# Close's products one chunk later, a third buffer for split's scaled copies, and a norm chain over three chunks

## The chip, the cores and the metric

The kernel runs on one core of one Trainium2 chip. The core has TensorE (PE, matmuls; its weight loads are listed as PEld), VectorE (DVE), ScalarE (ACT), GpSimd (POOL) and SyncE (SP), which here only issues DMAs. Each takes its own instructions in order, and they meet through semaphores. The metric is the device time of one execution in microseconds, as the median of several runs.

## The reference

Four images of 96 channels by 128 x 128 pixels, all in float32, pass through two layers, each added to its input after a group norm (`_gn`). The first is a state-space block: a projection and depthwise convolution to 192 channels, four scans over the pixels (`y0` to `y3`), their sum, a layer norm over the 192 channels at each pixel, and a projection back:

```python
ym = (y0 + y1 + y2 + y3).reshape(B, D_INNER, H, W)
yn = jnp.moveaxis(ym, 1, -1)
yn = (yn - mu) * jax.lax.rsqrt(var + 1e-05) * ln_w + ln_b
yn = jnp.moveaxis(yn, -1, 1)
return jnp.einsum('bdhw,cd->bchw', yn, out_w) + out_b[None, :, None, None]
...
x = x + _L0_conv_ref(_gn(x), ...)
```

The second layer splits its input by sign, makes convolution weights of the two halves ("attention"), and joins the results:

```python
xr, x1, x2 = _relu_split_norm(x, sc1, sc2, res_coef, nc1, nc2)
y1 = NORM_SCALE * _layer_norm(_attn_conv(x1, x2, aw1, aw2, aw3))
y2 = NORM_SCALE * _layer_norm(_conv2d(x2, w_conv2, K // 2)) * x1
y = jnp.concatenate([y1, y2], axis=1)
return xr + _conv2d(y, w_full, 0) + b_full[None, :, None, None]
```

## The kernel before

The program is one unrolled stream, written as Python generators that emit instructions and yield a cost in units. `co_run(left, right, pace)` takes a step of `left` and then as many steps of `right` as make up its cost times `pace`; this sets the order in which two tasks are emitted. In the first part, up to the end of the scan, `in_order` fixes on each engine the order of emission. After that the compiler's planner places instructions by its own estimate of times, with the order of emission as priority, so neighbours on one engine can change places. A tile in a pool with `bufs` buffers shares them with its successors; the writer of a new tile waits until all users of the tile that had the buffer are done (a WAR wait).

The stages are: projections and scan of all images; norm, count and split of image 0 beside the end of the scan; its maps by direct convolution (L2138), with image 1's norm beside it; then for each image the attention (`left`: products L1507 and L1522, evacuated by ACT as `odd` and `ends` at L1578 and by DVE at L1592 to L1600), beside a chain of light work (`right`): the norm of the next image, its count, and then its split in turn with the close of the image before. At the start of images 2 and 3 what is left of the light chain is emitted alone (`drain(light)`). Image 3 has a last stage of its own.

- **Norm** (`ssm_output`, L937). It walks over NS = 16 chunks of SN = 1024 pixels in six sections a round. `load_y` brings y, 96 partitions x 2 halves of the channels x 1024, from DRAM, into 3 buffers. `squares` (ACT, L956) and `sums` (PE, L966) make the sums over channels of y and of its squares; `rows` copies them out (ACT, L975) and turns them into `mq`, 8 partitions x 128, by two DMAs. `inverse` (DVE, L982 to L984), `roots` (ACT, L988) and `back` (DVE, L994 or L999; a store to `rd` on POOL's queue, L1001; a load of the input `xr` on SP's, L1003) give the inverse root, and `spread_out` (POOL's queue, L1009) loads it on all partitions as `r`. `projected` (PE, L1015) multiplies y by the output weights, a half of 512 pixels at a time, `scaled` (DVE, L1028, L1030) multiplies by r, `added` (POOL, L1036, L1038) adds xr, `counted` (DVE, L1042) takes statistics, and L1091 stores the chunk. Round c serves chunk c as `new`, c − 1 as `mid` and c − 2 as `old`. A round's six yields come to 8.2 units, and all of it to 149.6. For images 1 to 3 (`turned`) the sum lies in r's buffer, for image 0 in xr's. mq, xr and r have two buffers each.
- **Split** (`split_pieces`, L1219) makes two halves of the input for 32 pieces of four rows, and from each half six planes (`planes_of`, L1407): ACT makes two scaled copies, `x4` (L1430, three buffers) and `x2` (L1431, two buffers), and POOL forms the differences (L1439 to L1444, L1425).
- **Close** (`attn_output`, L2266) walks over NCH = 32 chunks of 512 pixels in three sections. `loads` brings `o`, `c2` and `xx` of the next chunk by three DMAs on SP's queue; ACT makes `x1` and `e` from xx (L2308), DVE finishes x1 (L2312), c2 (L2313) and e (L2316, L2317), PE adds two products into one PSUM bank (L2319 of o, L2320 of c2), DVE adds e (`added`, L2298 or L2300), and SP stores it (L2301). c2, xx, x1, e and o have two buffers each. `added` comes in the next chunk, ahead of its x1.

Norm's sums and projections, split's halves and close's products share two PSUM banks in `psr`.

Of the kernel before, what the change touches and what calls it, by code (L numbers as in the profile page):

```python
# [9 lines left out]
F32 = mybir.dt.float32  # L10
BF16 = mybir.dt.bfloat16
AF = mybir.ActivationFunctionType
# [5 lines left out]
C = 96  # L18
H = W = 128
L = H * W  # L20
CH = 512
NCH = L // CH
# [29 lines left out]
SN = 1024  # L52
# [17 lines left out]
def kernel(  # L70
# [211 lines left out]
    def part(ps, *shape):  # L282
        n = 1
        for d in shape[1:]:
            n *= d
        t = bank(ps)[: shape[0], :n]
        return t if len(shape) == 2 else t.rearrange("p (a b) -> p a b", b=shape[2])
# [649 lines left out]
    def ssm_output(b, yms, xnew, stats, ps, side, turned):  # L937
# [5 lines left out]
        with tc.tile_pool(name="c2", bufs=2, side=side) as p2:  # L943
            xb = x[b].rearrange("c h w -> c (h w)")
            ym = yms.rearrange("(j p) l -> p j l", j=2)
            rd = dram.tile([L], F32, name="rd")
            ys, sums_of, near, made = {}, {}, {}, {}

            def load_y(c):
                if c < NS:  # L950
                    ys[c] = p2.tile([C, 2, SN], F32, name="y", bufs=3)
                    nc.sync.dma_start(ys[c], ym[:, :, bass.ts(c, SN)])

            def squares(c, j):
                sq = p2.tile([C, SN], F32, name="sq")
# [55 lines left out]

            def projected(c, h):
                po = part(ps, C, CH)
                for j in range(2):
                    nc.tensor.matmul(  # L1015
                        po,
                        lhsT=outws[:, j],
                        rhs=ys[c][:, j, bass.ts(h, CH)],
                        start=(j == 0),
                        stop=(j == 1),  # L1020
                    )
                return po
# [18 lines left out]
                t = near[c][turned]  # L1041
                nc.vector.bn_stats(stats[:, 2 * c + h], t[:, bass.ts(h, CH)])  # L1042

            for c in range(3):
                load_y(c)
            yield 2.0
            for c in range(NS + 2):
                new, old = c < NS, c - 2 if c >= 2 else None
                mid = c - 1 if 1 <= c <= NS else None
                if old is not None:  # L1050
                    po = projected(old, 0)
                if mid is not None:
                    inverse(mid)
                if new:
                    squares(c, 0)
                yield 1.2
                if mid is not None:
                    roots(mid)
                if old is not None:
                    scaled(old, 0, po)  # L1060
                    po = projected(old, 1)
                    ys.pop(old)
                if new:
                    squares(c, 1)
                yield 1.4
                if mid is not None:
                    back(mid)
                if old is not None:
                    added(old, 0)
                    scaled(old, 1, po)  # L1070
                if new:
                    sums(c, 0)
                yield 1.4
                if new:
                    sums(c, 1)
                if old is not None:
                    added(old, 1)
                    counted(old, 0)
                    load_y(c + 1)
                yield 1.4  # L1080
                if new:
                    rows(c)
                if mid is not None:
                    xr = near[mid][0]
                    nc.scalar.activation(xr, xr, AF.Identity, bias=outbs)
                    spread_out(mid)
                if old is not None:
                    counted(old, 1)
                yield 1.4
                if old is not None:  # L1090
                    nc.sync.dma_start(xnew[:, bass.ts(old, SN)], near.pop(old)[turned])  # L1091
                yield 1.4

    def split_count(xnew, stats, keep, cnt, ps, side):
# [124 lines left out]
    def split_pieces(pools, xnew, x1d, x2d, keep, cnt, ps, side, planes, done):  # L1219
# [20 lines left out]
        def stored(i, m, h):  # L1240
            if planes:
                def then(pl):
                    store_planes(nc.sync, m, i * rows, rows, pl)
                    done[m is x2d] = (i + 1) * rows

                return planes_of(later, p2, h, rows, then, rows, bufs=(3, 2, 3), wait=1)
            at = (i * rows + 1) * PW
            return lambda: nc.scalar.dma_start(m[:, at : at + rows * PW], h)

# [1016 lines left out]
    def attn_output(pools, img, ps, side, share):  # L2266

        ob = out[img.b].rearrange("c h w -> c (h w)")  # L2270
        p1 = pools.enter_context(tc.tile_pool(name="f1", bufs=1, side=side))
        p3 = pools.enter_context(tc.tile_pool(name="f3", bufs=2, side=side))
        with_one = [p1.tile([128, CH], F32, name=f"o{k}")[0 : C + 1] for k in range(2)]
        for o in with_one:
            nc.gpsimd.memset(o[C : C + 1], 1.0)
        cost = 2.6 / 3 * share

        def loads(t):
            if t == NCH:
                return None  # L2280
            o = with_one[t % 2]
            got = [o]
            nc.sync.dma_start(o[0:C], img.od[:, bass.ts(t, CH)])
            for name, src in (("c2", img.c2d), ("xx", img.xnew)):
                y = p3.tile([C, CH], F32, name=name)
                nc.sync.dma_start(y, src[:, bass.ts(t, CH)])
                got.append(y)
            return got

        ahead = loads(0)  # L2290
        w1 = own_weights(img, ps, p1)
        s2, w2 = c2_weights(img, ps, p1)
        thr, scale, shift, up, low = (img.keep[n] for n in ("thr", "scale", "shift", "up", "low"))
        stt = nc.vector.scalar_tensor_tensor

        def added(t, pf, x1, e):
            if img.mapped:
                nc.vector.tensor_add(x1, pf, e)  # L2298
            else:
                nc.vector.tensor_add(plain(x1), pixels(pf), pixels(e))  # L2300
            nc.sync.dma_start(ob[:, bass.ts(t, CH)], x1)  # L2301

        summed = None
        for t in range(NCH):
            o, c2, xx = ahead
            x1, e = (p3.tile([C, CH], F32, name=n) for n in ("x1", "e"))
            for y, m, s in ((x1, scale[:, 0:1], shift[:, 0:1]), (e, up[:, 0:1], up[:, 1:2])):
                nc.scalar.activation(y, xx, AF.Identity, scale=m, bias=s)  # L2308
            yield cost
            if summed:  # L2310
                added(*summed)
            stt(x1, xx, thr, x1, ALU.is_gt, ALU.mult)  # L2312
            stt(c2, c2, s2[0:C, 0:1], x1, ALU.subtract, ALU.mult)  # L2313
            ahead = loads(t + 1)
            yield cost
            stt(e, xx, thr, e, ALU.is_gt, ALU.mult)  # L2316
            stt(e, xx, low[:, 0:1], e, ALU.mult, ALU.add)  # L2317
            pf = part(ps, C, CH)
            nc.tensor.matmul(pf, lhsT=w1, rhs=o, start=True, stop=False)  # L2319
            nc.tensor.matmul(pf, lhsT=w2, rhs=c2, start=False, stop=True)  # L2320
            summed = t, pf, x1, e
            yield cost
        added(*summed)

    class LastOutput:

# [363 lines left out]
```

## Time and profile before

| | us |
|---|---|
| median of 3 runs | 6667.03 |
| lowest and highest run | 6646.25, 6669.15 |
| profiled execution, its own time | 6658.24 |
| its span, first to last instruction | 6656.4 |

| stage (by its instructions in the trace) | window, us |
|---|---|
| norm of image 0, beside the scan | 2095 to 2360 |
| norm and count of image 1, beside the direct maps | 3215 to 3540 |
| norm of image 2, beside the attention of image 1 | 3950 to 4250 |
| split of image 2 with close of image 0 | 4311 to 4880 |
| norm of image 3, beside the attention of image 2 | 4880 to 5180 |
| split of image 3 with close of image 1 | 5260 to 5710 |
| close of image 2, beside the attention of image 3 | 5710 to 6130 |

The mean granted clock of PE is 0.879 of full speed over the span. The DMA engines moved 1198.45 MB, at a mean of 180 GB/s. A line of waits names the engine and the line that waited, what released it, the total, the number of times and the longest. In a line of a group the part after the first bar is its busy time and its mean in ns, and that after the second the idle time of the engine just ahead of it, with what ended it.

### The profile page before, as it was taken

The page shows a single profiled execution, that of the slowest core. Times are in us where ns is not written, and L with a number is a line of the kernel's source. Part 1 is how long each engine was busy: PE and PEld are TensorE (multiplying, and loading weights), DVE is VectorE, ACT ScalarE, POOL GpSimd, SP SyncE. Part 2 cuts the span into 40 slices and gives each one's busy share as a digit, 9 for nine tenths or more (in the row PEclk, how much of TensorE's full clock was granted, in tenths as well). Part 3 has the DMA queues.
Part 4 walks back from the last instruction along what each step waited for, and adds up shares of the span by engine and source line. Part 5 has one row for each costly group of instructions (what it writes and reads, how often), then busy time and mean ns, then how long its engine had stood idle before and what let it go on. Part 6 is the DMA issues. An engine that isn't in the chain of part 4 may idle for free. (4 is left out here: it accounts for less than half of the span.)

```text
span 6656.4 us, 78702 instructions
## 1 busy us (share of the span) xinstructions
PE 5402.4 (81%) x23264; PEld 2361.0 (35%) x23264; DVE 4808.8 (72%) x7229; ACT 3931.9 (59%) x5141; POOL 3963.2 (60%) x4145
## 2 busy tenths in 40 slices
PE   6889978978887727999984778877869777888888
PEld 2333323322222103444332243444324444344553
DVE  3247878988998778889557555676755777788867
ACT  1257768777876676677324664655645655644542
POOL 2236758978787548889325684388454577533420
PEclk9999989988997758999987889887979888998989
DMA  7766777865766766765765757545756554755657
GB/s 164 176 157 176 208 212 195 226 181 170 225 186 171 213 183 207 212 187 179 202 181 156 202 152 189 156 130 161 212 158 164 154 144 133 228 152 157 182 148 213
DMA packets 972215, 1198.45 MB, mean 180 GB/s; under 512 B 221518, under 2 KB 801686, under 8 KB 959308
## 3 DMA queue, kind: packets, MB, share of 16 engines
q1 hardware_dynamic: 948172, 1138.48, 61.7%
q0 software_dynamic: 16208, 38.42, 2.1%
q10 hardware_dynamic: 7408, 16.53, 0.8%
q8 instruction: 187, 3.06, 0.2%
q14 instruction: 240, 1.97, 0.1%
HBM read 777.62 MB, written 345.58 MB: 169 GB/s over the span
## 5 line engine op out<-in xcount | busy, mean ns | idle before, releaser
L635 PE MATMUL bank<-y,wp 128*128 128x512 f32 (+3 forms) x3584 | 1312.3, 622 | 80.7 <-DMA y<-y 33.3
L868 POOL TENSOR_TENSOR y<-y,dl 128x1024 f32<-128x1024 f32 x384 | 1064.5, 2772 | 263.6 <-DVE dl L860 238.1
L835 POOL TENSOR_TENSOR dl<-dl,u 128x1024 f32<-128x1024 f32 x384 | 1015.1, 2643 | 246.6 <-ACT dA L811 123.0
L856 DVE TENSOR_TENSOR_SCAN dA<-dA,pBC 128x512 f32<-128x512 f32 x768 | 981.5, 1278 | 30.7
L1507 PE MATMUL two<-ya,wd 128*64 128x192 f32 (+3 forms) x2376 | 609.8, 434 | 170.1 <-ACT odd L1578 83.9
L749 PE MATMUL pBC<-xr,wbc 60*128 60x512 bf16 (+1 forms) x1536 | 461.6, 403 | 322.8 <-DVE dA L856 248.1
L635 PEld LDWEIGHTS bank<-y,wp 128*128 128x128 f32 (+3 forms) x3584 | 457.5, 168 | 747.2 <-issue 651.4
L2138 PE MATMUL bank<-y,wn 128*128 128x384 f32 (+5 forms) x2408 | 675.3, 505 | 57.9 <-DMA y<-x1d 28.5
L860 DVE TENSOR_TENSOR dl<-dA,pBC 128x512 f32<-128x512 f32 x768 | 528.1, 688 | 252.6 <-PE pBC L749 180.0
L1941 ACT COPY yb<-ya 64x768 f32<-64x768 f32 (+1 forms) x660 | 537.1, 814 | 200.7 <-PE two L1507 143.7
L678 ACT ACTIVATE dl<-pd,dtb 128x512 f32<-128x512 f32 x768 | 485.5, 684 | 191.4 <-PE pd L749 173.8
L1507 PE MATMUL two<-yb,wd 128*64 128x192 f32 (+3 forms) x2376 | 582.2, 416 | 0.2 <-ACT yb L1941 0.2
L839 DVE TENSOR_TENSOR pBC<-dl,pBC 128x512 f32<-128x512 f32 x768 | 527.6, 687 | 8.8 <-POOL dl L835 7.7
L1425 POOL TENSOR_TENSOR pl<-x 96x128 f32<-96x128 f32 (+1 forms) x1032 | 496.7, 494 | 0.0
L2138 PEld LDWEIGHTS bank<-y,wn 128*128 128x128 f32 (+3 forms) x2408 | 310.2, 168 | 352.4 <-issue 177.3
L811 ACT ACTIVATE dA<-dl,negA 128x1024 f32<-128x1024 f32 x384 | 420.3, 1141 | 2.3
L1507 PEld LDWEIGHTS two<-ya,wd 128*64 128x64 f32 (+1 forms) x2376 | 275.3, 175 | 405.8 <-issue 113.9
L2011 POOL COPY own<-ring 32x512 f32<-32x512 f32 (+1 forms) x198 | 221.3, 1152 | 287.4 <-DVE ring L1600 253.0
L749 PEld LDWEIGHTS <-wbc 60*128 60x128 bf16 (+1 forms) x1536 | 104.1, 96 | 763.0 <-issue 750.0
L678 ACT ACT_TABLE_LOAD x248 | 318.2, 1283 | 93.9 <-PE pd L749 81.9
L1507 PEld LDWEIGHTS two<-yb,wd 128*64 128x64 f32 (+1 forms) x2376 | 304.7, 175 | 157.7 <-issue 49.8
L1507 PE MATMUL two<-ya,wa 128*96 128x384 f32 (+1 forms) x528 | 235.2, 530 | 111.0 <-DMA ya<-vp 57.5
(324 smaller groups left out, 10067.8 us busy)
## 6 DMA issues: line engine op xcount, KB each, us to landing
u<-zb SPq DMA_DIRECT2D x192, 1024.0 KB
yms<-y SPq DMA_DIRECT2D x96, 512.0 KB
y<-yms SPq DMA_DIRECT2D x64, 768.0 KB
ya<-vp SPq DMA_DIRECT2D x120, 336.0 KB
y<-y SPq DMA_DIRECT2D x128, 258.2 KB
zb<-z SPq DMA_DIRECT2D x64, 512.0 KB
xn<-xnew SPq DMA_DIRECT2D x80, 384.0 KB
ya<-x1p SPq DMA_DIRECT2D x90, 336.0 KB
```

The costliest lines, as they stand in the source:

```text
L635: nc.tensor.matmul(blocks(pz[p:e]), lhsT=ws[k][:, d, c : c + e - p], rhs=window(ys[k], at, d, n), start=(i == 0), stop=(i == len(terms) - 1),)
L678: nc.scalar.activation(dst, src, AF.Softplus, bias=bias)
L749: nc.tensor.matmul(p, lhsT=w[rows], rhs=xr[rows, at : at + CH], start=True, stop=True)
L835: nc.gpsimd.tensor_mul(t, t, u_view(n))
L839: nc.vector.tensor_mul(p, live[n]["dl"][:, bass.ts(half, CH)], p)
L856: nc.vector.tensor_tensor_scan(h, h, p, init, ALU.mult, ALU.add)
L860: nc.vector.tensor_mul(live[n]["dl"][:, sl], live[n]["dA"][:, sl], live[n]["C", half])
L868: nc.gpsimd.tensor_add(v, v, t.rearrange("p (a b) -> p a b", b=W))
L1425: op(to[i], x, y)
L1507: nc.tensor.matmul(of(to[p:e], r), lhsT=w[:, i, c : c + e - p], rhs=tiles(t[k][PAIR[i]][:, SLOT[i]], o, r), start=(k == 0), stop=False,)
L1941: nc.scalar.copy(yb[k][64 * h - 64 : 64 * h, :, :n], ya[k][0:64, :, h * TN : h * TN + n])
L2138: nc.tensor.matmul(pc[p:e, :n].rearrange("p (h w) -> p h w", w=W), lhsT=w[:, c : c + e - p], rhs=v[:, :, 0:W], start=(i == 0), stop=(i == ...
```

## The change

In the norm, y has two buffers for the squares and the sums, loaded a whole round ahead. A second read, `load_half`, brings y again in halves of 512 pixels (`yh`, two buffers of half the size) for `projected`. A round now serves four chunks: `new` c, `mid` c − 1, `far` c − 2 and `old` c − 3. `inverse`, `roots`, `back` and `spread_out` stand in other sections, `rows` and the first `counted` in the last; the second `counted` comes in the next round. A round costs 7.8 units, there is one more, and the whole is 153.3. In the split, x2 has three buffers. In the close the two products of a chunk come at the start of the next one, `added` behind that chunk's c2, and `loads` a section later.

```diff
@@ ssm_output
-            ys, sums_of, near, made = {}, {}, {}, {}
+            ys, again, sums_of, near, made = {}, {}, {}, {}, {}
             def load_y(c):
                 if c < NS:
-                    ys[c] = p2.tile([C, 2, SN], F32, name="y", bufs=3)
+                    ys[c] = p2.tile([C, 2, SN], F32, name="y")
                     nc.sync.dma_start(ys[c], ym[:, :, bass.ts(c, SN)])
+            def load_half(i):
+                if i < NCH:
+                    again[i] = p2.tile([C, 2, CH], F32, name="yh")
+                    nc.sync.dma_start(again[i], ym[:, :, bass.ts(i, CH)])
...
             def projected(c, h):
                 po = part(ps, C, CH)
+                y = again.pop(2 * c + h)
...
-                        rhs=ys[c][:, j, bass.ts(h, CH)],
+                        rhs=y[:, j],
...
-            for c in range(3):
+            for c in range(2):
                 load_y(c)
-            yield 2.0
-            for c in range(NS + 2):
-                new, old = c < NS, c - 2 if c >= 2 else None
+                load_half(c)
+            yield 4.0
+            late = []
+            for c in range(NS + 4):
+                new = c < NS
                 mid = c - 1 if 1 <= c <= NS else None
+                far = c - 2 if 2 <= c <= NS + 1 else None
+                old = c - 3 if 3 <= c <= NS + 2 else None
+                if c > NS + 2:
+                    yield 1.1
+                    late.pop()()
+                    return
+                if far is not None:
+                    back(far)
                 if old is not None:
                     po = projected(old, 0)
-                if mid is not None:
-                    inverse(mid)
                 if new:
+                    if c:
+                        load_y(c + 1)
                     squares(c, 0)
-                yield 1.2
-                if mid is not None:
-                    roots(mid)
+                yield 1.1
                 if old is not None:
                     scaled(old, 0, po)
                     po = projected(old, 1)
-                    ys.pop(old)
+                if late:
+                    late.pop()()
                 if new:
                     squares(c, 1)
-                yield 1.4
+                yield 1.3
                 if mid is not None:
-                    back(mid)
+                    inverse(mid)
+                if far is not None:
+                    spread_out(far)
                 if old is not None:
                     added(old, 0)
                     scaled(old, 1, po)
...
                     sums(c, 1)
                 if old is not None:
                     added(old, 1)
-                    counted(old, 0)
-                    load_y(c + 1)
-                yield 1.4
+                    load_half(2 * old + 2)
+                yield 1.3
+                if mid is not None:
+                    roots(mid)
+                if far is not None:
+                    xr = near[far][0]
+                    nc.scalar.activation(xr, xr, AF.Identity, bias=outbs)
+                if old is not None:
+                    load_half(2 * old + 3)
+                yield 1.3
                 if new:
                     rows(c)
-                if mid is not None:
-                    xr = near[mid][0]
-                    nc.scalar.activation(xr, xr, AF.Identity, bias=outbs)
-                    spread_out(mid)
                 if old is not None:
-                    counted(old, 1)
-                yield 1.4
-                if old is not None:
-                    nc.sync.dma_start(xnew[:, bass.ts(old, SN)], near.pop(old)[turned])
+                    counted(old, 0)
+                    nc.sync.dma_start(xnew[:, bass.ts(old, SN)], near[old][turned])
+                    late.append(lambda old=old: (counted(old, 1), near.pop(old)))
                 yield 1.4
@@ split_pieces
-                return planes_of(later, p2, h, rows, then, rows, bufs=(3, 2, 3), wait=1)
+                return planes_of(later, p2, h, rows, then, rows, bufs=(3, 3, 3), wait=1)
@@ attn_output
-        def added(t, pf, x1, e):
+        def multiplied(o, c2):
+            pf = part(ps, C, CH)
+            nc.tensor.matmul(pf, lhsT=w1, rhs=o, start=True, stop=False)
+            nc.tensor.matmul(pf, lhsT=w2, rhs=c2, start=False, stop=True)
+            return pf
+        def added(pf, t, x1, e):
...
-        summed = None
+        behind = None
         for t in range(NCH):
             o, c2, xx = ahead
...
+            if behind:
+                pf = multiplied(*behind[0])
             yield cost
-            if summed:
-                added(*summed)
             stt(x1, xx, thr, x1, ALU.is_gt, ALU.mult)
             stt(c2, c2, s2[0:C, 0:1], x1, ALU.subtract, ALU.mult)
+            if behind:
+                added(pf, *behind[1])
+            yield cost
             ahead = loads(t + 1)
-            yield cost
             stt(e, xx, thr, e, ALU.is_gt, ALU.mult)
             stt(e, xx, low[:, 0:1], e, ALU.mult, ALU.add)
-            pf = part(ps, C, CH)
-            nc.tensor.matmul(pf, lhsT=w1, rhs=o, start=True, stop=False)
-            nc.tensor.matmul(pf, lhsT=w2, rhs=c2, start=False, stop=True)
-            summed = t, pf, x1, e
+            behind = (o, c2), (t, x1, e)
             yield cost
-        added(*summed)
+        pf = multiplied(*behind[0])
+        yield cost
+        added(pf, *behind[1])
```

## The prediction

> **What bounds the kernel now.** I read the shares first, then windows cut at the stages, then the waits of TensorE (PE) in those windows, last the groups of single lines.
>
> ```profile
> PE 5402.4 (81%) x23264; PEld 2361.0 (35%) x23264; DVE 4808.8 (72%) x7229; ACT 3931.9 (59%) x5141; POOL 3963.2 (60%) x4145
> ...
> 2095.00:2360.00 265.00, 191.25 (x498) 46.53 (x497) 186.23 (x250) 172.14 (x188) 146.09 (x103) 0.67 0.74 210
> 3215.00:3540.00 325.00, 274.64 (x1027) 113.48 (x1024) 160.20 (x417) 114.06 (x176) 76.47 (x130) 0.89 0.68 182
> 3950.00:4250.00 300.00, 259.87 (x1442) 124.47 (x1444) 167.22 (x308) 142.26 (x186) 139.78 (x183) 0.91 0.64 171
> 4311.00:4880.00 569.00, 443.40 (x2050) 230.23 (x2048) 408.31 (x667) 328.21 (x502) 399.55 (x773) 0.81 0.58 164
> 4880.00:5180.00 300.00, 244.18 (x1316) 113.05 (x1316) 163.88 (x303) 138.28 (x180) 140.84 (x171) 0.89 0.62 166
> 5260.00:5710.00 450.00, 343.45 (x1860) 198.07 (x1861) 335.98 (x504) 248.39 (x383) 350.54 (x659) 0.82 0.51 147
> 5710.00:6130.00 420.00, 374.15 (x1751) 186.67 (x1749) 338.80 (x548) 226.19 (x315) 159.35 (x261) 0.93 0.61 176
> ```
>
> Columns of a window: length, busy time of PE, PE's weight loads, DVE, ACT and POOL, granted clock, DMA share, GB/s. Windows 1, 2, 3 and 5 hold the norm of images 0 to 3, windows 4 and 6 split beside close (images 2 and 0, then 3 and 1), window 7 mostly the close of image 2. PE leads, but is idle 74, 50, 40, 126, 56, 107 and 46 us there: 499 us, all that the change can win. Between 2440 and 3215 us and in the attention alone nothing is touched.
>
> ```profile
> PE bank L2320 <- DVE c L2313: 54.5, 17, 15.5
> ...
> PE bank L2320 <- DVE c L2313: 33.0, 11, 8.5
> PE two L1507 <- ACT odd L1578: 28.4, 7, 9.8
> ...
> PE bank L2320 <- DVE c L2313: 22.2, 16, 4.6
> ...
> PE bank L966 <- ACT sq L956: 23.5, 9, 4.5
> ...
> PE bank L966 <- DMA y<-yms: 18.6, 2, 14.8
> ```
>
> These are PE's waits (total us, times, longest) in windows 4, 6, 7, 1 and 5. Close's second product waits for c2: 54.5 + 33.0 + 22.2 = 109.7 us, 44 times. PE works in order, so the attention's products stand behind it.
>
> ```profile
> L2312 DVE SCALAR_TENSOR_TENSOR x<-xx,kept,x 96x512 f32<-96x512 f32 x96 | 150.5, 1567 | 69.4 <-ACT x L2308 63.4 <-DMA out<-x 5.4
> L1431 ACT ACTIVATE x<-half 96x264 f32<-96x264 f32 x192 | 81.6, 425 | 198.5 <-POOL pl L1444 198.2
> L982 DVE TENSOR_TENSOR mq<-mq 8x128 f32<-8x128 f32 x64 | 42.0, 656 | 160.0 <-DMA mq<-st 136.4 <-DMA yc<-x1p 23.5
> ```
>
> Each ends in the idle time ahead of it: c2's own operand is slow (L2312 has a mean of 1567 ns, a median of 748, a maximum of 11016), split's second scaled copy stalls ACT for 198 us, norm's first step on mq stalls DVE for 160 us.
>
> [...] one shape (L1015) takes 590 to 1170 ns, and the clock is lowest (0.81, 0.82) where PE waits most. [...] from the end of xx's issue to its first reader there are never under 2.8 us.
>
> **Close.** Nothing is added; the two products move from the third section of a chunk to the first of the next, the add behind x1's and c2's two DVE operations (1.5 us at 748 ns), and the three loads one section later. A section lasts 5.8, 6.3 and 2.9 us in the three closes (96 starts of L2308). c2 is then made two sections ahead of its product, 5.8 to 12.6 us, more than all but one of the 44 waits: I take 109.7 us off PE's list. What is late next:
> - DVE still loses the time in L2312. PE runs ahead only until the attention wants its next PSUM pair, freed by the same ACT and DVE queues. Give back 40%: +44 (between 0 and 110).
> - xx has a section less. I paired the 96 xx issues with their L2308 in time: the lead has a median of 12.6, 12.2 and 6.7 us. Taking a section off each lead, and letting ACT wait where less than 3.1 us is left, gives +87 us of ACT idle. ACT is 54 to 58% busy, so I pass 30% on: +26 (0 to 87).
> - [...] I take −10 (−20 to 0).
>
> Net −110 + 44 + 26 − 10 = −50, between −130 and +87. On SP the out store (L2301) is now behind a later add, and the loads behind that store; PE's WAR release of o and c2 keeps its two sections.
>
> **Third buffer.** One more x2 lets ACT write a copy three halves behind POOL's reading instead of two. x4 has three already, so the next limit is L1430, one instruction earlier. ACT's wait was 68.1 + 69.2 + 14.1 us in windows 4, 6, 7; half should go. What reaches PE is `odd` coming late, 7.9 + 6.7 and 28.4 + 5.8 us in windows 4 and 6, with other causes too; a quarter: −12 (−49 to +5[...]).
>
> **Norm.** PE's waits that belong to it, windows 1, 2, 3, 5: for sq 23.5 + 1.3 + 7.9 = 32.7, for y 3.2 + 7.8 + 2.1 + 18.6 = 31.7, for r (L1028, L1030) 18.2; 82.6 together. Distances between a step and its user, in the yields' units (one is 1.8 us: L956 advances 14.8 us a chunk of 8.2 units in window 3):
> - mq's DMA to its first DVE step 2.8 to 3.8; that step to the root 1.2 to 2.7; sums to rows 1.4 to 2.6; xr's load to its bias 2.8 to 5.1; r's load to scaled 4.0 to 6.5. ACT's waits ahead of L988 (139.6 us), L975 (115.2) and L1085 (59.3), and DVE's 144.6 for mq and 62.4 for r, should fall by well over half. The root no longer stands ahead of the second square: sq −22, r −10.
> - y to squares 4.2 to 7.8: −32. But projected now reads yh, loaded 4.0 and 3.8 units ahead, where y had 4.2 and was late 17 times on ACT and 7 on PE: give back half, +16. The WAR releases are early: yh's by a product two sections before.
> - The slot of r: from the store that frees it to spread_out 6.8 to 3.8 units, about 7 us. POOL waited 21.2 us for this store before; three times that stalls POOL, not PE, but attention's L2011 stands behind: +5. For image 0 the slot of xr frees only when counted has run, one section after its load is issued, so SP stands there 2.5 us a chunk, ahead of the scan's prefetches, which are several steps early: +3.
> - DVE comes earlier to the scan's and attention's steps: window 1 has 30.4 us of PE waiting for dA (L856); −5.
> - y is read twice: 12.6 MB more an image, 128 issues instead of none, some 0.4 us each on SP. At 171 to 210 GB/s the DMA share of these windows goes from 0.62–0.74 to about 0.8–0.92; +5 for later landings (0 to 40).
> - A 19th round: 153.3 units for 149.6, 3.7 × 1.8 = 7 us an image of one stream, shown only where that stream is emptied alone (4805 to 4880): +5.
>
> Net −22 − 10 − 32 + 16 + 5 + 3 − 5 + 5 + 5 = −35, between −88 and +60.
>
> **Sum.** −50 − 12 − 35 = −97. From this I take 10 off for the planner: after image 0's part instructions are placed by its own estimate (in the timeline at 4061 us L966's products of y precede L1015's, those of sq follow), so a section isn't a fixed place. −87 on 6658.24 (span 6656.4 and 1.8 around it) is 6571. The median shown, 6667.03, is 8.8 higher, and its runs spread over 22.9; I forecast 6575.
>
> **Rivals.**
> - *Waits change their name, no change.* PE stops waiting for c2 and waits for `odd` and the PSUM pairs instead. For: window 4 has DVE and POOL at 72 and 70%, and DVE waits 47.6 us for `odd` there. Against: window 7, with POOL at 38%, shows c2 waits too. Close gives 10 and norm 10: about 6645. Chance 0.22. That placement undoes the delay (a product put back beside its operand) ends here too.
> - *Everything is won.* 110 + 20 from close, 60 from norm, 20 from split: about 6475. Chance 0.08.
> - *Slower: close's loads become the loop.* xx's landing (3.1), L2308 (0.8), x1 (0.75), c2 (0.74), the add (1.05), the store's issue (0.4), three issues (1.4) now follow one another, as the loads stand on SP behind the store of an add that stands behind this chunk's c2: 8.2 us a chunk with no queue ahead. Window 7's chunk lasts 8.8 us, so 0.6 us of queueing decides. If a load loses two sections, the same pairing gives 293 us of ACT idle instead of 87; 75% of it on PE against the 110 won is +110, less 20 from the rest: about 6760. For: SP's stores already hang behind DVE (89.8 us at L2301 in window 7). Against: the planner may issue the loads ahead of the store, since o and c2 are free by then. Chance 0.25.
>
> **Numbers.** The forecast has 0.45 (own range 6530 to 6620). About 0.5% (33 us) is what a measurement of this kernel tells from no change. Faster: 0.45, 0.08 and a little of the first rival, 0.55; same 0.18; slower 0.27. The range, 6465 to 6750, leaves out the worse half of the slower case and a little at the lower end.
>
> **What would show it.** L2320's wait for c2 under 15 us; L2308's wait for xx 12.1 before, under 100; L1431's for POOL under 110; L982's for mq under 70; L966's for y near nothing and L1015 with a new wait for yh of 10 to 25; windows 4 and 6 shorter by 20 us each, clock above 0.84. Wrong: L1507's waits for `odd` up by more than 60 us, L2308's above 200, or the closes' chunk above 8.8 us in the last.

## The result, and the profile after

The changed kernel takes 6745.56 us (median of 4 runs, 6743.37 to 6765.72) against 6666.57 us for the kernel before: ratio 1.0132, interval [1.0104, 1.016]. The change is slower by about 1.3%; the forecast was 1.4% faster. A second measurement beside its parts gave 1.0133. The profiled execution has a span of 6742.2 us and a granted clock of 0.874, before 6656.4 us and 0.879. The engines' busy times in it:

```profile
PE 5408.8 (80%) x23264; PEld 2368.4 (35%) x23264; DVE 4727.9 (70%) x7229; ACT 3933.0 (58%) x5140; POOL 3985.0 (59%) x4145
```

PE is busy as long as before (5402.4 us), so what was lost is idle time of PE.

The stage windows of after, in the order of the seven shown for the kernel before (length, busy time of PE, weight loads, DVE, ACT and POOL, clock, DMA share, GB/s):

```profile
2095.00:2400.00 305.00, 186.67 (x506) 48.25 (x506) 180.06 (x264) 175.90 (x195) 148.89 (x104) 0.63 0.81 224
3240.00:3600.00 360.00, 283.94 (x1078) 122.07 (x1078) 165.53 (x393) 99.71 (x152) 91.42 (x126) 0.87 0.76 201
4060.00:4380.00 320.00, 270.50 (x1514) 136.74 (x1512) 167.34 (x329) 145.87 (x192) 138.68 (x170) 0.90 0.72 189
4440.00:4985.00 545.00, 428.92 (x1935) 216.30 (x1931) 373.83 (x646) 316.99 (x483) 404.40 (x763) 0.83 0.62 172
4990.00:5300.00 310.00, 272.94 (x1515) 136.95 (x1507) 165.22 (x327) 145.26 (x191) 144.62 (x179) 0.90 0.76 199
5365.00:5800.00 435.00, 344.11 (x1789) 189.39 (x1789) 300.07 (x494) 247.06 (x380) 352.59 (x647) 0.82 0.56 153
5800.00:6220.00 420.00, 368.41 (x1751) 184.46 (x1752) 340.97 (x553) 227.86 (x315) 161.20 (x258) 0.94 0.63 178
```

The windows are cut at the stages by eye, so single lengths are good to some 10 us. Windows 1 and 2, the norms of images 0 and 1, are 40 and 35 us longer with hardly more work in them (in window 2, PE has 51 more products): PE is idle 118 and 76 us there instead of 74 and 50. Their DMA share is 0.81 and 0.76, before 0.74 and 0.68. The windows with close and split (4 and 6) are shorter, by 24 and 15 us, and the norms of images 2 and 3 (3 and 5) 20 and 10 us longer, with more of the attention's products in them.

PE's waits of after in window 1 (first line), window 2 (second) and over the whole run (the rest):

```profile
PE bank L1021 <- DMA yh<-yms: 81.4, 14, 13.5
...
PE bank L1021 <- DMA yh<-yms: 24.8, 9, 8.4
...
PE bank L1021 <- DMA yh<-yms: 107.0, 26, 13.5
PE bank L2318 <- DVE c L2338: 82.2, 43, 7.5
PE two L1526 <- ACT odd L1597: 82.1, 34, 7.1
```

L1021 is the projection's product. It waits 107 us for the half of y that is read again, nearly all of it in the norms of images 0 and 1. Close's second product (L2318) still waits for c2, 82.2 us in 43 waits, before 109.7 in 44.

Groups with what ended the idle time ahead of each, one of before (L1430 is L1449 of after) and three of after:

```profile
L1430 ACT ACTIVATE x<-half 96x528 f32<-96x528 f32 x192 | 122.3, 637 | 72.4 <-DVE half L1275 36.3 <-POOL pl L1425 26.4 <-DMA wful<-in_w_full 8.6
...
L1449 ACT ACTIVATE x<-half 96x528 f32<-96x528 f32 x192 | 122.4, 638 | 137.9 <-POOL pl L1444 90.3 <-POOL pl L1462 14.4 <-DVE pl L1492 13.4
L1450 ACT ACTIVATE x<-half 96x264 f32<-96x264 f32 x192 | 81.5, 424 | 137.2 <-POOL pl L1463 120.5 <-DVE half L1294 13.3 <-DVE two L1617 2.1
L987 DVE TENSOR_TENSOR mq<-mq 8x128 f32<-8x128 f32 x64 | 28.9, 451 | 101.1 <-DMA mq<-st 100.4 <-DMA vp<-pl 0.7
```

L987 and L1450 wait less than before (101.1 us for 160.0, 137.2 for 198.5), but L1449 waits longer by as much as L1450 gains (137.9 for 72.4).

I also paired the n-th step of the main task in both traces (DVE's scan, ACT's copies in the direct maps, its `odd` copies in the attention). Differences in us from the profile of before, which itself lies some 10 us below its median. In the two rows of the scan, what a run was already late when image 0's norm began (0, 5, 7, 12 and 6 us, in the order of the columns) is taken off; in the other rows it is not. Each column is one profile; that of halves_only is 22 us below its median, the others at most 5.

```
                              after  norm_only  norm_image0  norm_image1  halves_only
end of image 0's norm           +33        +34          +36           +7          +24
end of the scan                 +41        +41          +43           +8          +22
direct maps, step 96 of 130     +42        +48          +57          +17          +35
direct maps, step 120           +80        +88          +62          +48          +75
attention, step 8 of 176        +85        +89          +43          +38          +67
attention, step 72              +59        +65          +26          +45          +52
attention, step 168             +88        +66          +16          +39          +61
```

In after the whole loss is there before the attention starts; from there it changes by some tens of us in both directions and ends where it was. In norm_only and norm_image0 a part of the delay is made up in the attention (89 to 66 us, 43 to 16), in norm_image1 nothing (38 to 39).

### The profile page after: what moved, and what is told of

Its sections match the earlier page's. It is cut to its first block, busy times and chain, and to the rows that moved or that the text cites. A ratio compares the mean times of both kernels' runs of the same rounds, so it can differ in the third digit from the quotient of the medians.

```text
span 6742.2 us, 79037 instructions
## 1 busy us (share of the span) xinstructions
PE 5408.8 (80%) x23264; PEld 2368.4 (35%) x23264; DVE 4727.9 (70%) x7229; ACT 3933.0 (58%) x5140; POOL 3985.0 (59%) x4145
## 5 line engine op out<-in xcount | busy, mean ns | idle before, releaser
L1526 PE MATMUL two<-ya,wd 128*64 128x192 f32 (+3 forms) x2376 | 613.8, 428 | 194.9 <-ACT odd L1597 75.7
L1526 PE MATMUL two<-yb,wd 128*64 128x192 f32 (+3 forms) x2376 | 587.0, 412 | 23.5 <-ACT yb L1960 23.5
L1444 POOL TENSOR_TENSOR pl<-x 96x128 f32<-96x128 f32 (+1 forms) x1032 | 515.8, 513 | 0.0
L1526 PEld LDWEIGHTS two<-ya,wd 128*64 128x64 f32 (+1 forms) x2376 | 279.3, 172 | 415.6 <-issue 105.2
L1021 PE MATMUL bank<-yh,outws 96*96 96x512 f32 x512 | 298.7, 730 | 107.1 <-DMA yh<-yms 107.0
L1526 PEld LDWEIGHTS two<-yb,wd 128*64 128x64 f32 (+1 forms) x2376 | 307.2, 173 | 189.9 <-issue 63.9
L1294 DVE SCALAR_TENSOR_TENSOR half<-xn,kept,bank 96x512 f32<-96x512 f32 x192 | 141.3, 739 | 279.2 <-POOL pl L1460 101.6
```

The lines of the kernel that those rows point to most:

```text
L1444: op(to[i], x, y)
L1526: nc.tensor.matmul(of(to[p:e], r), lhsT=w[:, i, c : c + e - p], rhs=tiles(t[k][PAIR[i]][:, SLOT[i]], o, r), start=(k == 0), stop=False,)
```

## The experiments

All ratios are to the kernel before; in the diffs the lines with a minus are those of the kernel that the text names as its base.

### The parts alone

Three kernels with one or two of the three functions from the changed kernel, the others from before: norm_only (`ssm_output`), close_only (`attn_output`), close_and_split (`attn_output` and the third buffer).

> Norm's part of the change alone (chain over three chunks, y read again by halves); close and the third buffer stay as before. Theory A, the loss is norm's second read (PE waits for yh, 107 us in the trace of after, 81 of it beside image 0's scan): ratio to before 1.011 to 1.016, PE's wait for yh again 95 to 120 us. Rival B, the loss comes from close or from the third x2 buffer: ratio below 1.004.

> Close's part alone. Theory A: the engines' order keeps product and add beside c2, so nothing moves: ratio 0.997 to 1.002, PE's wait for c at the second product 80 to 110 us in all. The forecast's step: ratio 0.991 to 0.994 and the wait below 20 us. Rival B: ratio above 1.004.

> Everything but norm's part: close's products and the third buffer of the scaled copies. Theory A: ratio 0.995 to 1.000, since all of the loss is norm's. Rival B: 1.004 or more.

norm_only: 1.0086 [1.0067, 1.0106], with 105.0 us of PE waiting for yh. close_only: 1.0005 [0.9993, 1.0017]. close_and_split: 0.9996 [0.9983, 1.0009]. The forecast's largest gain, 50 us from close, isn't there. Most of the loss is norm's, but less than the 1.011 expected; 0.5% is left over, to which I come back.

Why close wins nothing is seen in two waits of close_only, of PE and of DVE (whole run), and PE's in close_pinned (last line):

```profile
PE bank L2299 <- DVE c L2319: 140.2, 48, 12.4
...
DVE x L2318 <- ACT x L2314: 129.0, 43, 11.1
```

```profile
PE bank L2316 <- DVE c L2337: 133.7, 45, 10.5
```

PE waits longer for c2 than before (109.7 us), though the product is emitted later. c2 itself comes later: its first operation on DVE waits 129.0 us for ACT's x, 63.4 before. In the order in which TensorE's instructions were built, the product moved by a median of 6 instructions (quartiles 0 and 12) where a chunk holds 20 to 37, counted in the attention's products. close_pinned asks whether that is the planner's doing:

```diff
         def multiplied(o, c2):
             pf = part(ps, C, CH)
+            first = len(traced())
             nc.tensor.matmul(pf, lhsT=w1, rhs=o, start=True, stop=False)
             nc.tensor.matmul(pf, lhsT=w2, rhs=c2, start=False, stop=True)
+            pinned(first)   # may not stand ahead of the last TensorE instruction emitted before
```

> Close's part alone, with each chunk's two products held in the engine's order behind the last TensorE instruction that was emitted before them; the orders of VectorE and SyncE are the same as in close's part alone. Theory E, the planner puts the product forward to its operand and the delay is undone: PE's wait for c falls from 140 to below 50 us, ratio 0.990 to 0.996. Rival F, c2 itself comes late in the order of VectorE, and a later product only stands where the wait was: wait for c above 80 us or as much in another wait, ratio 0.997 to 1.003.

1.0001 [0.9991, 1.0012]. Pinning moved no product by more than one place, so the planner had not put them forward: theory E falls. F holds: in the built orders, counted in the attention's instructions of the same engine, a chunk's products come later by 0.26 of a chunk (mean of the 96 chunks), and so do c2 on DVE (0.29) and x on ACT (0.27). The product gained no distance from its operand. From norm_only to after the three shifts are 0.30, 0.29 and 0.28, so it is no different beside the new norm, though there PE's wait for c2 (82.2 us) and DVE's for x (49.1) are shorter than before. The change also emits the loads of o, c2 and xx a section later, which may be why the planner puts x and c2 later; no run has the later products with the loads in their old place.

### Is it the second read or the longer chain?

halves_only keeps norm's old chain over two chunks, and only reads y again by halves:

```diff
-                    ys[c] = p2.tile([C, 2, SN], F32, name="y", bufs=3)
+                    ys[c] = p2.tile([C, 2, SN], F32, name="y")
...
-                        rhs=ys[c][:, j, bass.ts(h, CH)],
+                        rhs=y[:, j],
...
                     counted(old, 0)
-                    load_y(c + 1)
+                    load_half(2 * old + 2)
+                    load_half(2 * old + 3)
```

> The norm of before, its chain over two chunks and the order of its sections, with y in two buffers and read a second time by halves for the projection, as in the change. Theory A, the second read is what costs: ratio to before 1.006 to 1.013, PE's wait for yh 60 us or more. Rival C, the longer chain and its order of sections cost, and the read is paid for by DMA engines that are free: ratio below 1.003 and PE's wait for yh below 30 us.

1.0117 [1.0097, 1.0138], with 79.0 us of PE waiting for yh. The second read, with the two buffers of y and of the halves that go with it, costs 78 us (0.0117 of 6666); with the longer chain added the loss is 0.86%, so the chain seems to give some 20 us back (0.0031 of 6666; the two intervals overlap a little). No run has the longer chain without the second read. Rival C falls.

### Which image?

The change's norm for one image or two, the norm of before for the others:

```diff
-            yield from ssm_output(self.b, yms, self.xnew, ...)
+            made = ssm_output_late if self.b == 0 else ssm_output   # then b == 1, then b > 1
+            yield from made(self.b, yms, self.xnew, ...)
```

> Norm's part of the change for image 0 alone; images 1 to 3 keep the norm of before. From the trace of after: the scan of the other images, which runs beside it, comes 35 to 45 us late and the end with it, ratio 1.004 to 1.007. Rival D, the delay is made up before the end because attention waits for something else: below 1.002.

> Norm's part for image 1 alone. From the trace of after: the direct maps beside it come 35 to 50 us late, ratio 1.004 to 1.008, and PE's wait for y<-x1d at the direct maps' product rises from 28 to 50 us or more, since both loads are queued on SP. Rival D: below 1.002.

> Norm's part for images 2 and 3 alone, which run beside attention. From the trace of after, whose main task neither gains nor loses there: ratio 0.997 to 1.002. The forecast's reading of norm (35 us won over all images) would have here 0.994 to 0.997.

Image 0: 1.0014 [1.0004, 1.0024]. Image 1: 1.0052 [1.0033, 1.0071]. Images 2 and 3: 0.998 [0.997, 0.9989], a small gain. Image 0 was a surprise: its scan is 43 us late, as in the whole change (table above), and most of that is made up by the attention's end, so rival D holds for it. For image 1 the delay stays, but not by the wait that was expected. PE's waits over the whole run, of norm_image1 and then of before:

```profile
PE bank L1178 <- DMA yh<-yms: 29.0, 7, 7.2
...
PE bank L2314 <- DMA y<-x1d: 28.6, 7, 13.7
```

```profile
PE bank L2138 <- DMA y<-x1d: 28.5, 7, 13.5
```

PE's wait for the direct maps' own load x1d is the same as before; what is new is that it stands 29.0 us at the halves themselves. The three ratios add up to 0.46%, norm_only is 0.86%: together the parts cost about 27 us more than their sum, a little more than the four intervals together leave open. The table shows where it comes from. At step 120 of the direct maps norm_only is no later than the two early norms added up (88 for 62 + 48); at the attention's step 168 it is (66 for 16 + 39). What is made up after image 0's norm alone is not made up with all norms changed; whether image 1's norm or those of images 2 and 3 prevent it, no run separates.

### Why the halves come late in image 0

SP's waits of after in window 1, and then those of before in its window 1:

```profile
SPq L1008 <- DMA xnew<-xr: 87.6, 12, 12.6
SPq L1109 <- POOL xr L1044: 25.8, 8, 7.0
...
SPq L1008 <- DVE xstats L1048: 16.4, 7, 3.2
```

```profile
SPq L1091 <- POOL xr L1038: 91.9, 13, 10.9
SPq L1003 <- DMA xnew<-xr: 37.7, 13, 6.0
```

SP stands 104 us ahead of xr's load (L1008, before L1003), whose buffer is freed by a store and by a count that is emitted a section later; the halves' loads are queued behind. Together with the stand at the chunk's own store (L1109, before L1091) that is 129.8 us, and it was 129.6 before: SP doesn't stand longer, it stands at another place, with other loads behind it. Two kernels take the stand at xr away. norm_x_last is norm_only with the halves' loads ahead of xr's (xr's bias moves a section later too):

```diff
                     load_half(2 * old + 2)
+                    load_half(2 * old + 3)
+                if far is not None:
+                    load_x(far)          # was in back(far), three sections earlier
                 yield 1.3
...
-                if old is not None:
-                    load_half(2 * old + 3)
```

norm_xr3 has a third buffer for xr in image 0, and the built order of all five engines is that of norm_only:

```diff
-                st = p2.tile([128, CH], F32, name="st", bufs=1)
+                st = p2.tile([128, SN], F32, name="st", tag="sq")[:, 0:CH]     # image 0
-                xr = p2.tile([C, SN], F32, name="xr")
+                xr = p2.tile([C, SN], F32, name="xr", bufs=3)                  # image 0
```

> Norm's part alone, with SP's order changed: both loads of the halves stand ahead of xr's load, which moves three sections later in its round, behind the count that frees its buffer; its bias moves one section later. Theory A1, SP stands at xr's load (88 + 16 us in image 0's norm) and the halves behind it come late: PE's wait for yh beside image 0's scan falls from 81 to below 25 us, and the ratio to before from about 1.013 to 1.005 to 1.009 (image 1's 43 us stay). Rival A2, the halves are late because of the traffic itself (DMA share 0.81 there against 0.74): the wait stays above 60 us, ratio within 0.003 of norm's part alone.

> Norm's part alone, and in image 0 a third buffer for xr (room for it comes from st, which there takes a buffer of sq); the order of the instructions on every engine is the same as in norm's part alone. Theory A1, the load of xr at the head of SP's queue waits for its buffer (90 + 17 us in image 0's norm) and the halves stand behind it: that wait goes, PE's wait for yh beside image 0's scan falls from 87 us to below 25, the scan's delay from 41 us to below 15, ratio from 1.0086 to about 1.004. Rival A2, the DMA engines are full there (share 0.83 to 0.97): SP's wait goes, but the halves still land late, PE's wait for yh stays above 50 us and the ratio within 0.003 of norm's part alone.

norm_x_last 1.01 [1.0081, 1.0119], norm_xr3 1.0066 [1.0052, 1.0079]. Waits of norm_xr3 in image 0's norm (2050 to 2420 us), PE's and then SP's:

```profile
PE bank L1021 <- DMA yh<-yms: 71.5, 12, 12.5
```

```profile
SPq L957 <- PE bank L1021: 34.5, 13, 3.8
...
SPq L957 <- PE pBC L749: 13.4, 7, 3.0
```

SP no longer stands for xr's buffer (before 89.5 + 17.0 us in norm_only, now none for the store and 0.4 for the count), and yet PE still waits 71.5 us for yh where norm_only has 86.6. In norm_x_last it waits 54.1. The scan is still 23 and 28 us late, where norm_only has 41. norm_x_last is no faster than norm_only for it (1.01 for 1.0086). So SP's queue was a part only. Once xr no longer holds SP up, SP stands 34.5 us at the halves themselves (L957), for PE to free their buffers. One chunk of norm_xr3 shows the rest: SP's issues, one of PE's waits, and the window around them.

```profile
2224.66 0.37 SPq L1008 DMA_DIRECT2D xr<-in_x  x1
2225.14 0.67 SPq L952 DMA_DIRECT2D y<-yms  x1
2225.86 0.53 SPq L766 DMA_DIRECT2D u<-zb  x1
2226.48 3.83 SPq L957 DMA_DIRECT2D yh<-yms  x2
```

```profile
2240.24 3.73 PE L1021 MATMUL bank<-yh,outws 96*96 96x512 f32 x4 [11.56 <-DMA yh<-yms]
```

```profile
2200.00:2300.00 100.00, 57.52 (x196) 16.40 (x188) 60.01 (x90) 61.50 (x68) 53.92 (x39) 0.70 0.96 256
```

Within 6 us SP asks for 384 KB of xr, 768 of y, 1024 of the scan's u and 2 × 384 of the halves, 2.9 MB, and the halves are last. At the 256 GB/s of this window that is, as an estimate, 11 to 12 us; PE's product starts 15.6 us after the first of these issues. The DMA share is 0.96, so the engines have hardly any room. Both theories have a share. norm_yh3 adds to norm_x_last a third buffer of the halves in image 0, each half asked for one projection earlier:

```diff
-                    load_half(2 * old + 2)
-                    load_half(2 * old + 3)
+                    load_half(2 * old + first)        # first is 3 in image 0, 2 in the others
+                    load_half(2 * old + first + 1)
```

> Norm's part alone with xr's load behind the halves as in norm_x_last, and in image 0 a third buffer of the halves (room from st, which takes a buffer of sq there), so that each half is asked for one projection earlier. Theory G, in image 0 two buffers turn once a chunk and each half stands behind y and u (2.2 MB) in SP's DMA queue between its buffer's release and its landing: PE's wait for yh beside image 0's scan falls from 54 us to below 20, the scan's delay from 28 us to below 12, ratio 1.004 to 1.007. Rival A2, the DMA engines are simply full: the wait stays at 40 us or more, or turns into a wait for y or u, and the delay stays above 20 us.

The wait falls to 36.7 us and the scan's delay from 28 to 20, neither as far as G has it, and the kernel is at 1.0112 [1.0091, 1.0132]. So of norm_only's 86.6 us the order on SP's queue and the third buffer take 50 away, with the same bytes read; 36.7 are left, at a DMA share of 0.96 between 2200 and 2300 us. Half of the 50 comes back under other names: PE's wait for dA rises from 42.6 to 56.2 us, that for sq from 6.4 to 18.2. As with norm_image0, what is won in image 0 doesn't reach the end.

traffic_only reads y again into a buffer that nobody uses:

```diff
+            def again(i):
+                for j in range(2):
+                    yh = p2.tile([C, CH - 16], F32, name="yh", bufs=1)
+                    nc.sync.dma_start(yh, ym[:, j, i * CH : (i + 1) * CH - 16])
```

> The kernel before, which in addition reads y a second time in pieces of 96 x 496 that nobody uses (same bytes within 3%, on SP's queue, one small buffer of its own): the traffic and SP's issues without anything that waits for them on PE. Theory A1 (slots and order in SP's queue): ratio below 1.003. Rival A2 (the traffic itself): 1.006 or more, the scan beside image 0's norm 20 us late or more. Between the two: each has a share.

1.0364 [1.034, 1.0388], but this doesn't measure the traffic: with one buffer each load waits for the one before, and SP stood 154.9 us at these loads in image 0's norm, with y behind them. The scan is 94 us late; how much of that is SP's standing and how much the bytes, this run can't tell. What the bytes alone cost stays open.

### Why image 1 is late

Beside image 1's norm run the direct maps, whose loads are on SP's queue too. In norm_yh_on_act ScalarE issues the halves:

```diff
-                    nc.sync.dma_start(again[i], ym[:, :, bass.ts(i, CH)])
+                    nc.scalar.dma_start(again[i], ym[:, :, bass.ts(i, CH)])
```

> Norm's part alone with the loads of the halves issued by ScalarE instead of SyncE, in all images. Theory H, what costs in image 1 is that SP stands for PE at these loads with the direct maps' loads behind it: the direct maps' delay in image 1's stretch falls from 43 us to below 20, PE's wait for y<-x1d and y<-x2d there from 45 us to below 30, and in image 0 the halves no longer stand behind y and u: ratio 1.002 to 1.006. Rival A2, the traffic: direct maps' delay above 30 us, ratio 1.008 or more. Rival I, ScalarE stands in SyncE's place: its own wait for PE at these loads above 60 us, ratio 1.008 or more.

PE's waits between 3240 and 3720 us in norm_only, and between 3240 and 3700 us in norm_yh_on_act:

```profile
PE bank L2157 <- DMA y<-x1d: 39.5, 4, 13.3
...
PE bank L1021 <- DMA yh<-yms: 17.8, 8, 4.1
...
PE bank L2157 <- DMA y<-x2d: 5.7, 1, 5.7
```

```profile
PE bank L2157 <- DMA y<-x1d: 18.0, 3, 12.6
PE bank L2157 <- DMA y<-x2d: 8.3, 1, 8.3
...
PE bank L1021 <- DMA yh<-yms: 4.6, 2, 2.5
```

1.0059 [1.0044, 1.0075]. The direct maps lose 22 us between steps 96 and 120 instead of 40, and their wait for y falls from 45.2 to 26.3 us: H holds to about half. In norm_only SP stood 30.4 us at the halves for PE in this stretch, with the maps' loads queued behind; with ScalarE issuing, PE's waits for x1d, x2d and the halves add up to 30.9 us, as before (31.5 between 3204 and 3615 us), where norm_only has 63.0. So these waits explain about half of the delay. The other half is not in them. PE's busy time in these stretches is 350.0 us for 1289 products at a clock of 0.86 and a DMA share of 0.76, before 337.2 us for 1292 at 0.88 and 0.65; this profile is the slowest of its six executions, so that too stays open. The ratio is not image 1's alone, since ScalarE issues in all four images: in image 0 the scan is 23 us late instead of 41. Rival I falls: ScalarE stood 18 us in all at these loads, 4.7 at the longest.

### The half per cent left over

> The whole change, beside the same runs of the kernel before as its parts. If the parts add up (norm 1.0086, close with the third buffer 0.9996): 1.007 to 1.010. If close and the third buffer, free on their own, cost beside the new norm: 1.011 to 1.015, as measured first.

> Norm's part with the third buffer of the scaled copies, without close's part. The whole change is 1.0133 where the parts' sum would be 1.008. If the third buffer is what costs beside the new norm: 1.012 to 1.015; if close's part does: 1.007 to 1.010.

> Norm's part with close's part, without the third buffer. If close's part is what costs beside the new norm: 1.012 to 1.015; if the third buffer does: 1.007 to 1.010. If both this run and norm_split are near 1.010, it is neither alone.

> Norm's part for images 2 and 3 with close's part. The two are 0.998 and 1.0005 alone. If what close's part costs beside the new norm (0.5%) comes from the norms of images 2 and 3, in whose stretches the closes run: 1.002 to 1.005. If it comes from the norms of images 0 and 1, or from how late those leave the rest: 0.997 to 1.000.

> Norm's part for images 2 and 3 with the third buffer of the scaled copies, close as before: the parts that have cost nothing or won so far. If they add up (0.998 and, by norm_split against norm_only, 0.999): 0.995 to 0.999. If the third buffer or the order that the planner finds takes it back: 0.999 or more.

after_again 1.0133 [1.0116, 1.015], norm_split 1.0074 [1.0059, 1.0089], norm_close 1.0139 [1.0121, 1.0156], images23_close 1.0031 [1.0019, 1.0043], images23_split 0.9963 [0.9948, 0.9978]. Close's part, free with the old norm, costs 0.5% with the new one, and the norms of images 2 and 3 are enough for it: 0.998 becomes 1.0031. They don't run at the same moment: the closes lie in windows 4, 6 and 7, those norms in 3 and 5. How the one reaches the other isn't shown. PE's waits of norm_images23 and of images23_close over the run:

```profile
PE bank L2496 <- DVE c L2489: 107.3, 42, 13.1
PE two L1683 <- ACT odd L1754: 67.6, 32, 7.6
...
PE two L1683 <- ACT ends L1754: 24.8, 15, 5.0
```

```profile
PE bank L2475 <- DVE c L2495: 90.3, 43, 7.5
PE two L1683 <- ACT odd L1754: 83.6, 33, 7.5
...
PE two L1683 <- ACT ends L1754: 35.7, 13, 13.8
...
PE two L1683 <- DMA wa<-ring: 15.7, 3, 9.5
```

The wait for c2 loses 17 us; the attention's products wait 16 us more for `odd`, 11 for `ends` and 14 for the load of `wa` (1.4 us in norm_images23). That is where some of PE's time went, not why: no run takes it away. images23_split, with the third buffer, the new norm for images 2 and 3 alone, and close as before, beats both kernels: 6645.69 us (median of 9 runs) against 6666.64 for the kernel before beside it.

## Why the forecast was wrong, by its steps

The forecast's parts come to −97 us; measured were +79 at first and +89 in after_again. By the experiments norm is off by 92 us, close by 84 and the third buffer by 4.

**Close, −50.** Failed at its first term. I took the whole 109.7 us off PE's list because c2 would be made two sections ahead of its product. The product moved by one section (it had stood one behind c2 already), and c2 moved too, by the same quarter of a chunk, with ACT's x. Alone, close gave +3 us (1.0005, interval −5 to +11). The term for ACT's wait for xx (+26) was not needed: it was 7.4 us in after, 12.1 before. The first rival, waits that change their name, comes nearest to what happened to close, and with the new norm the exchange was a loss of 34 us (1.0031 less 0.998). The clock's term (−10) was my guess, which no trace or run of this case bears out: the waits stayed (140.2 us for c2 in close_only), and the mean granted clock is 0.877 in close_only, 0.879 before. The forecast read the clock as lowest (0.81, 0.82) where PE waits most; its own first window has 0.67, with the largest idle share of all, 74 of 265 us.

**Third buffer, −12.** Right in place and about right in size, as far as the runs can tell: norm_split against norm_only gives −8 us, images23_split against norm_images23 −11, both with overlapping intervals. As the forecast said, the limit moved one instruction earlier: L1450's wait fell from 198.5 to 137.2 us, that of L1449 on the same half rose from 72.4 to 137.9. In after the two together are no shorter (275.1 us for 270.9); in norm_split they are (222.1, norm_only 295.2).

**Norm, −35.** This is the step that turned the sign: yh's "give back half, +16". The chain's own terms were right in direction for three waits: PE's for sq fell from 33.3 to 13.2 us, for y from 31.7 to 5.3, DVE's for mq from 136.4 to 100.4 (I had wanted under 70), and the chain seems worth some −20. They were wrong for others: PE's wait for r rose from 18.2 to 20.7 us instead of losing 10, and of the waits of ACT that "should fall by well over half" none fell (139.6 to 156.0 us ahead of the root, 115.2 to 155.0 at the copy of the sums, 59.3 to 62.0 at xr's bias). But projected now reads yh, and for that I gave back half of y's wait, +16, since its distance in yields was the same; PE waited 107 us, and the second read without the longer chain cost 78. A distance in yields is worth what the queue leaves of it: in image 0 the halves land behind 2.2 MB (the chunk of norm_xr3 above), through DMA engines that I had myself put at 0.8 to 0.92 and priced at +5. The slot of xr was put at +3 for 2.5 us a chunk, the wait for the count. That took 16.4 us, 1.0 a chunk; the store, which the term leaves out, took 87.6 (37.7 before), and a third buffer won 13 us (1.0086 less 1.0066, with overlapping intervals). The direct maps' loads behind SP's wait for yh I didn't see at all.

**Slower, by another way.** The slower rival, a loop through close's loads, didn't happen; its sign for `odd` (over 60 us more at L1526) didn't show, with 82.1 us for 92.2, and the last close's chunk takes 8.5 us (8.6 before, by the starts of L2308, where the forecast has 8.8). The range held the time, 6745.56 us, by luck and by 4 us: it had been widened for that rival and for the read's bound of +40, and the second measurement, 6758.95 us, lies outside.

**The sum.** Norm +57 (1.0086), of which image 1 alone 35, image 0 alone 9, images 2 and 3 −13, and the rest only when they are together; close with it +34; the third buffer −8: 83 of the 89 us that after_again shows. What stays open: what the bytes of the second read cost without its place in the queue, why the norms cost more together than apart, what the other half of image 1's delay is, and why close's part costs together with the new norms of images 2 and 3.

## What to carry to other kernels

A buffer that is paid for with a second read can move its cost to the queue, as here (78 us lost in halves_only, with 79.0 us of PE waiting for yh): before pricing it, add up the bytes that stand ahead of the new load, divide by the GB/s of that very window, and ask which loads stand behind the place where the issuing engine waits for a buffer. The same change was a gain of 0.2% beside the attention and a loss of 0.5% beside the direct maps, and the DMA share alone doesn't tell which: in after it is 0.72 and 0.76 in the one case and 0.76 in the other. And a product emitted later helps only if its operand isn't late with it (with close alone the products came 0.26 of a chunk later, c2 0.29, at a ratio of 1.0005): follow the operand's own wait one step back first.

## What the runs showed that I had not expected

A delay isn't a loss: image 0's norm put the scan 43 us back, and 9 us of it were left at the end. Two harmless parts were not harmless together: 1.0005 and 0.998 made 1.0031. And a load that nobody uses, with a single buffer on a shared queue, cost 3.6%.
